# A Mamba and attention kernel: the tails of C copied by ScalarE from PSUM, and a later C product in one slot of sixteen

## The chip, the cores and the metric

One NeuronCore of a Trainium2 chip runs the whole program. The metric is the device time of one execution in microseconds, as the median of repeated runs. Five engines work side by side, each through its own instructions in order: TensorE (PE in the profile), VectorE (DVE), ScalarE (ACT), GpSimd (POOL) and SyncE (SP), which here only issues DMAs. They wait for each other through semaphores.

## The reference

Two layers over x of 4 batches, 512 channels, 64 x 64 positions (L = 4096). The second layer is a linear attention with 8 heads. The first is a group norm, a layer norm, and then, for each of 4 chunks of 128 channels, a Mamba block with 256 inner channels and 16 states:

```python
xz = einsum(x, in_proj_w); xi, z = split(xz)
xc = silu(causal_conv4(xi)); dt, Bs, Cs = split(einsum(xc, x_proj_w))
dt = softplus(einsum(dt, dt_proj_w) + dt_proj_b)
h  = exp(dt_t * A) * h + (dt_t * x_t) * B_t      # per channel and state, over t
y  = sum over states of h * C_t
y  = (y + xc * D_param) * silu(z);  out = einsum(y, out_proj_w)
```

The step that matters here is y: every state's h is multiplied with its row of C, and the 16 states are summed.

## The kernel before, in words

**Tiling.** The sequence is cut into NT = 8 tiles of T = 512 positions. A *step* n is one batch, tile and chunk: 4 x 8 x 4 = 128 steps. A step has 256 channels x 16 states = 4096 recurrences, which fill 32 scans of 128 partitions x 512 positions. On the partitions lie 32 channels times 4 states. A *slot* is two scans (SLOTS = 16 a step, 2048 in all), a *pair* of slots makes one h tile [128, 4, 512] (hs, two buffers): the even slot of the pair is jj = 0, the odd one jj = 1.

**What a slot issues** (slot, L725). GpSimd forms bx = (dt x) * B two slots ahead (drive, L717 and L721; three buffers). ScalarE forms dA = exp(dt * A) three scans ahead into three PSUM banks (decay, L708 and L713, LEAD = 3), so that decay k + 3 can start when scan k has freed its bank. VectorE scans (L739). After the first scan of an even slot the previous pair is finished: VectorE multiplies columns 0 to 383 of its h by C, in place (product, L756 and L759), which it reads from a PSUM bank; TensorE fills that bank for the next pair (c_row, L702: one selecting matmul of the bf16 parts of the C rows, CUT = 384 columns wide; one buffer) and folds the finished h over the states into y (fold_states, L761). At the end of an odd slot GpSimd saves the last column (L750) and multiplies the tail, columns 384 to 511, by C (L751). [...] its part of C comes as an SBUF tile c_sb, which four DMAs for each pair spread from DRAM (c_tail, L697, through for_states, L685; two buffers), issued one slot before the pair begins. The rows of B come in the same way, three pairs ahead (b_row, L692), and the step times and dt x in eight DMAs of 256 KB for each half step (spread, L633, at slots 1 and 9).

**Order of the work around it.** The order within each engine is the order in which the program writes the instructions. After each slot, after() (L1109) adds the other stages at fixed slots: first what later() has put off to this slot, then among others the softplus with its two ScalarE table loads at slot 3 (L1127), the gates on GpSimd at slots 1 and 9, the inputs of step n + 2 at slots 3 and 5 to 9 (inputs, L579: the convolution's matmuls and the z matmuls into banks pc and pz, evacuated by ScalarE a slot later, L592 and L608), their Silu at slot 10 (L1048: a table load, one activation over [128, 2048], and a table load back to exp), their x, B, C projection from slot 12 (mixers, L642). Between these come pieces of the layer norms, the output projection and the previous batch's attention, as long as TensorE's budget for the slot lasts.

**The C rows.** mixers puts dt, B and three copies of the C rows into one bank pd, copies B and C to SBUF and by DMA to DRAM (rows_out, L658), and splits the 384 columns that TensorE will select into three bf16 parts (L663 to L669): a copy, then twice a matmul that subtracts it and a copy of what is left.

Of the kernel before, what the change touches and what calls it, by code (L numbers as in the profile page):

```python
# [8 lines left out]
F32 = mybir.dt.float32  # L9
# [5 lines left out]
P = 128  # L15
# [9 lines left out]
def kernel(  # L25
# [60 lines left out]
    def later(n, what):  # L86

        done = []

        def both():  # L90
            what()
            done.append(True)

        if now[0] is None:
            both()
        else:
            due.append((now[0] + n, both))
        return done
# [22 lines left out]
    def mm(out_, lhsT, rhs, abreast=1, **how):  # L121

        work["mm"] += (0.25 if rhs.dtype == BF16 else 1.0) * rhs.shape[-1] / T / abreast
        nc.tensor.matmul(out_, lhsT, rhs, **how)  # L124
# [250 lines left out]
    def bc(v, n):  # L375
        return v.unsqueeze(1).to_broadcast([P, n, v.shape[-1]])
# [190 lines left out]
    def shifted_end(f, name):  # L567
        mv = small.tile([P, NC, 2], F32, tag="mv", name=f"mv_{name}", bufs=4)
        for v in range(2):
            nc.vector.tensor_reduce(mv[:, :, v], f[("sum", "square")[v]], AX.X, ALU.add)  # L570
        nc.gpsimd.tensor_scalar(mv, mv, 1.0 / L, None, ALU.mult)
        d2 = small.tile([P, NC], F32, tag="d2", name=f"d2_{name}")
        nc.gpsimd.tensor_tensor(d2, mv[:, :, 0], mv[:, :, 0], ALU.mult)
        nc.gpsimd.tensor_tensor(mv[:, :, 1], mv[:, :, 1], d2, ALU.subtract)
        nc.gpsimd.tensor_tensor(mv[:, :, 0], mv[:, :, 0], f["mv"][:, :, 0], ALU.add)
        return mv


    def inputs(f, xn, c, nm):  # L579

        xz = f["xz"] = wk.tile([P, 2, NH, T], F32, tag="xz", name=f"xz_{nm}", bufs=3)
        pc = [None] * NH

        def taps(e, ks):
            for k in ks:
                mm(
                    pc[e], w_cv[:, k, e * P : (e + 1) * P], xn[:, c, k : k + T],
                    start=(k == 0), stop=(k == NTAP - 1),
                )

        def take(e):
            nc.scalar.activation(xz[:, 0, e, :], pc[e], AF.Identity, bias=cb[:, e : e + 1])  # L592

        for e in range(NH):
            pc[e] = work_bank(f"pc_{nm}_{e}", 0)
            taps(e, range(NTAP // 2))
            yield
            taps(e, range(NTAP // 2, NTAP))
            later(1, lambda e=e: take(e))
            yield  # L600
        for e in range(NH):
            pz = work_bank(f"pz_{nm}_{e}", 0)
            mm(
                pz, w_z[:, e * P : (e + 1) * P], xn[:, c, NTAP - 1 : NTAP - 1 + T],
                start=True, stop=True,
            )

            later(1, lambda e=e, pz=pz: nc.scalar.copy(xz[:, 1, e, :], pz))  # L608
            yield

    def time_banks(f, nm):
# [30 lines left out]
    def mixers(f, nm):  # L642

        pd = work_bank(f"pd_{nm}", 0)
        for e in range(NH):
            mm(pd, w_xp[:, e, :], f["xz"][:, 0, e, :], start=(e == 0), stop=(e == NH - 1))
        yield
        f["both"] = wk.tile([P, 2, NH, T], F32, tag="dt", name=f"dt_{nm}", bufs=1)  # L650
        dtr = f["dtr"] = f["both"][0 : 2 * LANE, 1, NH - 1, :]
        nc.scalar.copy(dtr, pd[0 : 2 * LANE, :])
        b_rows = f["b_rows"] = dram.tile([NST, T], F32, tag="b_rows", name=f"b_rows_{nm}", bufs=3)
        c_rows = f["c_rows"] = dram.tile(
            [NST, T - CUT], F32, tag="c_rows", name=f"c_rows_{nm}", bufs=3
        )

        def rows_out():  # L658
            nc.sync.dma_start(b_rows, dtr[RANK : RANK + NST, :])
            nc.sync.dma_start(c_rows, dtr[LANE : LANE + NST, CUT:])  # L660

        later(1, rows_out)
        parts = f["parts"] = wk.tile([P, CUT], BF16, tag="parts", name=f"parts_{nm}", bufs=3)  # L663
        nc.scalar.copy(parts, pd[:, :CUT])
        for i in (2, 3):
            yield
            mm(pd[:, :CUT], minus, parts, start=False, stop=True, skip_group_check=True)
            yield
            nc.scalar.copy(parts[i * LANE :, :], pd[i * LANE :, :CUT])  # L669

# [12 lines left out]
    def for_states(dst, rows_, q):  # L685

        for k in range(KS):
            nc.sync.dma_start(  # L688
                dst[k * BLK : (k + 1) * BLK, :], rows_[q * KS + k, :].partition_broadcast(BLK)
            )  # L690
# [5 lines left out]

    def c_tail(g):  # L697
        n, e, q, _ = place(g)
        c_sb[g // JJ] = wk.tile([P, T - CUT], F32, tag="c_sb", name=f"c_sb_{g}", bufs=2)
        for_states(c_sb[g // JJ], fs[n]["c_rows"], q)  # L700

    def c_row(g):  # L702
        n, e, q, _ = place(g)
        got = ps_c.tile([P, CUT], F32, tag="c", name=f"c_all_{g}")
        mm(got, sel[:, q, :], fs[n]["parts"], start=True, stop=True)
        c_all[g // JJ] = got

# [17 lines left out]
    def slot(g, last, after):  # L725
        n, e, q, jj = place(g)
        b, t, c = steps[n]
        if g + 2 < last:
            drive(g + 2)
        if jj == 0:  # L730
            if g + 3 * JJ < last:
                b_row(g + 3 * JJ)
            hs[g // JJ] = wk.tile([P, NJ, T], F32, tag="h", name=f"h_{g}", bufs=2)
        elif g + 1 < last:
            c_tail(g + 1)
        h = hs[g // JJ]
        for i in range(2):
            j = jj * 2 + i
            nc.vector.tensor_tensor_scan(  # L739
                h[:, j, :], dAs.pop(2 * g + i), bxs[g][:, i, :],  # L740
                0.0 if t == 0 else st[:, c, e, q, j : j + 1], ALU.mult, ALU.add,
            )
            if 2 * g + i + LEAD < 2 * last:
                decay(2 * g + i + LEAD)
            if i == 0 and jj == 0 and g:
                product(g - 1)
                fold_states(g - 1, last)
        del bxs[g]
        if jj == JJ - 1:
            nc.gpsimd.tensor_copy(st[:, c, e, q, :], h[:, :, T - 1])  # L750
            nc.gpsimd.tensor_tensor(  # L751
                h[:, :, CUT:], h[:, :, CUT:], bc(c_sb.pop(g // JJ), NJ), ALU.mult
            )
        after()

    def product(g):  # L756

        own = hs[g // JJ][:, :, :CUT]
        nc.vector.tensor_tensor(own, own, bc(c_all.pop(g // JJ), NJ), ALU.mult)  # L759

    def fold_states(g, last):  # L761

# [43 lines left out]
    def attention(b, x1s, stats):  # L806
# [87 lines left out]

        kqn = wk.tile([P, NC, P], F32, tag="res", name=f"kqn_{b}", bufs=2)
        nc.gpsimd.memset(kqn, 0.0)
        nrm = small.tile([P, NC], F32, tag="nrm", name=f"nrm_{b}")
        nc.vector.tensor_reduce(nrm, kq, AX.X, ALU.add)
        nc.gpsimd.tensor_scalar(nrm, nrm, 1e-6, None, ALU.add)
        nc.vector.reciprocal(nrm, nrm)  # L900
# [145 lines left out]
        return inputs(fs[n], xn[b, t], c, names[n])  # L1046

    def silu(n):  # L1048
        nc.scalar.activation(fs[n]["xz"], fs[n]["xz"], AF.Silu)  # L1049

    ahead, late, rest, light = [], [], [], []

# [21 lines left out]
    silu(0)  # L1074
    run(mixers(fs[0], names[0]))
    b_row(0)
    c_tail(0)
    time_banks(fs[0], names[0])
    time_steps(fs[0], names[0])
    for v in range(2):  # L1080
# [160 lines left out]
```

## Time and profile before

| | us |
|---|---|
| runs before | 7912.8, 7906.63, 7911.72 (median 7911.72) |
| the profiled execution | 7900.44 |
| its span, first to last instruction | 7898.7 |
| busy: POOL, DVE, PE, ACT | 6894.4, 6908.9, 6434.6, 5509.8 |
| all 128 steps, first to last scan | 7301 |
| issue of one c_sb load on SP, median | 0.42 |
| c_sb load, issue to landing, median | 1.8 |

A line of a group reads: line of the kernel, engine, operation, output<-inputs, shapes, count, then busy time and the mean ns of one, then the engine's idle time just before such instructions and what ended it. Line 124 is the helper mm, through which all matmuls go, so matmuls are told apart by their tiles. In the timeline a row has the start, the duration and, in brackets, the idle time before it. Records of consecutive instructions on VectorE and ScalarE overlap by some hundredths of a microsecond. A wait for several things is put down to the one that came last.

### The profile page before, as it was taken

What the parts mean: (1) busy time and instruction counts of PE and PEld (TensorE: products, weight loads), DVE (VectorE), ACT (ScalarE), POOL (GpSimd) and SP (SyncE); (2) the same over time, 40 slices, a digit from 0 to 9 for tenths busy, and PEclk for the clock granted to TensorE, in tenths of its full rate; (3) what the DMA queues carried; (4) which work ended last, traced back from release to release, by engine and by line L of the source; (5) the groups of instructions that cost most, each with busy time, mean ns of one, the idle gap of its engine ahead of it and who ended that gap; (6) DMA issues with size and microseconds to landing.
All of it is one profiled execution on the core that took longest, in us unless ns stands there. A gap on an engine that the chain in (4) does not pass through costs nothing.

```text
span 7898.7 us, 90490 instructions
## 1 busy us (share of the span) xinstructions
PE 6434.6 (81%) x24834; PEld 2109.1 (27%) x24880; DVE 6908.9 (87%) x5650; ACT 5509.8 (70%) x8329; POOL 6894.4 (87%) x4649
## 2 busy tenths in 40 slices
PE   5676777677789888988788888888788888888599
PEld 1121212112223232322222223322122222322144
DVE  5999999999999999989999999998989999988500
ACT  4677777777777777777777777777777777777421
POOL 4999999999999999989999999999999999999500
PEclk7888888788899999999899999999889999999799
DMA  5676666666776666776766666777666666677402
GB/s 156 167 170 168 159 153 158 161 155 165 171 176 165 161 163 159 182 187 174 170 167 169 171 164 159 175 179 181 164 159 169 158 164 155 156 194 182 102 32 91
DMA packets 829184, 1265.87 MB, mean 160 GB/s; under 512 B 183912, under 2 KB 317560, under 8 KB 816384
## 3 DMA queue, kind: packets, MB, share of 16 engines
q1 hardware_dynamic: 804736, 1222.32, 61.5%
q0 software_dynamic: 16896, 33.56, 2.5%
q10 hardware_dynamic: 7040, 4.20, 0.2%
q8 instruction: 195, 3.19, 0.2%
q14 instruction: 317, 2.60, 0.1%
HBM read 1052.78 MB, written 206.57 MB: 159 GB/s over the span
## 4 chain that ended last, share of the span: by engine, by line
DVE 32%; PE 21%; DMA 13%; ACT 12%; issue 8%; POOL 7%; SPq 6%; POOLq 0%; DVEq 0%; ACTq 0%
DVE h L739 22%; DVE h L759 9%; DMA d_all<-d_rows 7%; PE pq L124 5%; POOL bx L721 5%; ACT dA L713 4%; PE pc L124 4%; SPq L688 3%; PE y L124 3%; PE pr L124 2%; SPq L639 2%; PE po L124 2%; DMA c_sb<-c_rows 2%; ACT xz L1049 2%; DMA b_all<-b_rows 2%
## 5 line engine op out<-in xcount | busy, mean ns | idle before, releaser
L721 POOL TENSOR_TENSOR bx<-d_all,b_all 128x1024 f32<-128x1024 f32 x2048 | 4824.4, 2369 | 157.7 <-DVE h L739 141.3
L739 DVE TENSOR_TENSOR_SCAN h<-dA,st,bx 128x512 f32<-128x512 f32 x3584 | 4358.0, 1264 | 372.5 <-ACT dA L713 164.4
L713 ACT ACTIVATE dA<-d_all,a_t 128x512 f32<-128x512 f32 x4096 | 2754.3, 687 | 1501.3 <-DVE h L739 1444.7
L759 DVE TENSOR_TENSOR h<-h,c_all 128x1536 f32<-128x1536 f32 x1024 | 1767.6, 1726 | 0.1
L751 POOL TENSOR_TENSOR h<-h,c_sb 128x512 f32<-128x512 f32 x1024 | 1301.1, 1271 | 227.2 <-DMA c_sb<-c_rows 125.1
L124 PE MATMUL y<-h,fold 128*32 128x512 f32 x8192 | 1271.6, 697 | 93.2 <-POOL h L751 88.6
L124 PE MATMUL c_all<-parts,sel 128*128 128x384 bf16 x1024 | 368.3, 360 | 1073.2 <-DVE h L759 1071.0
L124 PE MATMUL pc<-xn,w_cv 128*128 128x512 f32 x2048 | 1037.4, 640 | 118.7 <-DVE xn L414 63.9
L124 PE MATMUL pq<-w_qk,xa 128*128 128x512 f32 x2048 | 963.8, 604 | 7.8 <-issue 4.9
L739 DVE TENSOR_TENSOR_SCAN h<-dA,bx 128x512 f32<-128x512 f32 x512 | 591.8, 1204 | 88.5 <-ACT dA L713 62.7
L124 PEld LDWEIGHTS <-sel 128*128 128x128 bf16 x1280 | 126.8, 99 | 1716.1 <-DVE h L759 1519.5
L124 PEld LDWEIGHTS pc<-xn,w_cv 128*128 128x128 f32 x2048 | 386.5, 199 | 736.4 <-issue 418.0
L124 PEld LDWEIGHTS pq<-w_qk,xa 128*128 128x128 f32 x2048 | 396.6, 195 | 443.7 <-issue 425.4
L124 PE MATMUL pr<-xb,m 128*128 128x512 f32 x1024 | 481.8, 608 | 12.3 <-DMA xb<-x 7.0
L124 PE MATMUL pp<-xn,w_pr 128*128 128x512 f32 x1024 | 477.9, 597 | 4.8 <-DVE xn L414 4.8
L124 PEld LDWEIGHTS y<-h,fold 128*32 128x32 f32 x8192 | 170.3, 114 | 661.9 <-issue 322.4
L124 PE MATMUL y<-xz,dg 32*32 32x512 f32 x2048 | 335.8, 731 | 0.0
L781 POOL TENSOR_TENSOR xz<-xz 128x512 f32<-128x512 f32 x256 | 325.9, 1273 | 5.9 <-ACT xz L778 5.8
L832 ACT ACTIVATE kq<-pq 128x512 f32<-128x512 f32 x256 | 150.6, 588 | 253.3 <-PE pq L124 252.5
L124 PE MATMUL pd<-xz,w_xp 128*128 128x512 f32 x512 | 318.3, 753 | 7.8 <-ACT xz L1049 7.8
L628 POOL TENSOR_TENSOR dt<-dt,xz 128x1024 f32<-128x1024 f32 x128 | 302.5, 2363 | 22.5 <-ACT dt L620 22.5
L124 PE MATMUL pz<-xn,w_z 128*128 128x512 f32 x512 | 273.2, 625 | 9.7 <-ACT xz L608 8.2
(177 smaller groups left out, 5981.2 us busy)
## 6 DMA issues: line engine op xcount, KB each, us to landing
d_all<-d_rows SPq DMA_DIRECT2D x2048, 256.0 KB, 6.6
b_all<-b_rows SPq DMA_DIRECT2D x4096, 64.0 KB, 2.2
d_rows<-dt SPq DMA_DIRECT2D x256, 512.0 KB, 3.7
c_sb<-c_rows SPq DMA_DIRECT2D x4096, 16.0 KB, 1.8
xs<-in_x_dram SPq DMA_DIRECT2D x32, 1024.0 KB, 6.1
xn<-in_x_dram SPq DMA_DIRECT2D x32, 1024.0 KB, 6.2
xr<-in_x_dram POOLq DMA_DIRECT2D x32, 1024.0 KB, 10.2
x<-xr SPq DMA_DIRECT2D x32, 1024.0 KB, 4.2
```

What stands on the lines that cost most here:

```text
L124: nc.tensor.matmul(out_, lhsT, rhs, **how)
L628: nc.gpsimd.tensor_tensor(f["both"][:, 1], f["both"][:, 0], f["xz"][:, 0], ALU.mult)
L639: nc.sync.dma_start(d[k * BLK : (k + 1) * BLK, v], src)
L688: nc.sync.dma_start(dst[k * BLK : (k + 1) * BLK, :], rows_[q * KS + k, :].partition_broadcast(BLK))
L713: nc.scalar.activation(dAs[k], fs[n]["d_all", e][:, 0, j, :], AF.Exp, scale=a_t[:, e, j, q : q + 1])
L721: nc.gpsimd.tensor_tensor(bxs[g], fs[n]["d_all", e][:, 1, jj * 2 : jj * 2 + 2, :], bc(b_all[g // JJ], 2), ALU.mult)
L739: nc.vector.tensor_tensor_scan(h[:, j, :], dAs.pop(2 * g + i), bxs[g][:, i, :], 0.0 if t == 0 else st[:, c, e, q, j : j + 1], ALU.mult, AL ...
L751: nc.gpsimd.tensor_tensor(h[:, :, CUT:], h[:, :, CUT:], bc(c_sb.pop(g // JJ), NJ), ALU.mult)
L759: nc.vector.tensor_tensor(own, own, bc(c_all.pop(g // JJ), NJ), ALU.mult)
L781: nc.gpsimd.tensor_tensor(f["xz"][:, 1, e, :], f["xz"][:, 1, e, :], f["xz"][:, 0, e, :], ALU.mult)
L832: nc.scalar.activation(qk[i], pq, AF.Relu)
L1049: nc.scalar.activation(fs[n]["xz"], fs[n]["xz"], AF.Silu)
```

## The change

Four things. The parts of C, their subtracting matmuls and the selecting matmul become 512 columns wide, so that the bank c_all holds the whole row. c_tail becomes one ScalarE copy of columns 384 to 511 of that bank to c_sb (one buffer), issued in the pair's own odd slot behind the decay that follows its first scan; the DRAM tile c_rows, its write and the four loads for each pair go. At slot 10 of each step the product and the fold of the pair before are issued behind the slot's second scan. The second z bank is not copied to SBUF any more: Silu is done in two activations, over the three quarters that lie in SBUF and from the bank. Three small buffers become single.

```diff
@@ -569,7 +569,7 @@
         for v in range(2):
             nc.vector.tensor_reduce(mv[:, :, v], f[("sum", "square")[v]], AX.X, ALU.add)
         nc.gpsimd.tensor_scalar(mv, mv, 1.0 / L, None, ALU.mult)
-        d2 = small.tile([P, NC], F32, tag="d2", name=f"d2_{name}")
+        d2 = small.tile([P, NC], F32, tag="d2", name=f"d2_{name}", bufs=1)
         nc.gpsimd.tensor_tensor(d2, mv[:, :, 0], mv[:, :, 0], ALU.mult)
         nc.gpsimd.tensor_tensor(mv[:, :, 1], mv[:, :, 1], d2, ALU.subtract)
         nc.gpsimd.tensor_tensor(mv[:, :, 0], mv[:, :, 0], f["mv"][:, :, 0], ALU.add)
@@ -605,7 +605,9 @@
                 start=True, stop=True,
             )
 
-            later(1, lambda e=e, pz=pz: nc.scalar.copy(xz[:, 1, e, :], pz))
+            if e + 1 < NH:
+                later(1, lambda e=e, pz=pz: nc.scalar.copy(xz[:, 1, e, :], pz))
+            f["pz"] = pz
             yield
 
     def time_banks(f, nm):
@@ -651,22 +653,18 @@
         dtr = f["dtr"] = f["both"][0 : 2 * LANE, 1, NH - 1, :]
         nc.scalar.copy(dtr, pd[0 : 2 * LANE, :])
         b_rows = f["b_rows"] = dram.tile([NST, T], F32, tag="b_rows", name=f"b_rows_{nm}", bufs=3)
-        c_rows = f["c_rows"] = dram.tile(
-            [NST, T - CUT], F32, tag="c_rows", name=f"c_rows_{nm}", bufs=3
-        )
 
         def rows_out():
             nc.sync.dma_start(b_rows, dtr[RANK : RANK + NST, :])
-            nc.sync.dma_start(c_rows, dtr[LANE : LANE + NST, CUT:])
 
         later(1, rows_out)
-        parts = f["parts"] = wk.tile([P, CUT], BF16, tag="parts", name=f"parts_{nm}", bufs=3)
-        nc.scalar.copy(parts, pd[:, :CUT])
+        parts = f["parts"] = wk.tile([P, T], BF16, tag="parts", name=f"parts_{nm}", bufs=3)
+        nc.scalar.copy(parts, pd)
         for i in (2, 3):
             yield
-            mm(pd[:, :CUT], minus, parts, start=False, stop=True, skip_group_check=True)
+            mm(pd, minus, parts, start=False, stop=True, skip_group_check=True)
             yield
-            nc.scalar.copy(parts[i * LANE :, :], pd[i * LANE :, :CUT])
+            nc.scalar.copy(parts[i * LANE :, :], pd[i * LANE :, :])
 
 
 
@@ -696,12 +694,12 @@
 
     def c_tail(g):
         n, e, q, _ = place(g)
-        c_sb[g // JJ] = wk.tile([P, T - CUT], F32, tag="c_sb", name=f"c_sb_{g}", bufs=2)
-        for_states(c_sb[g // JJ], fs[n]["c_rows"], q)
+        c_sb[g // JJ] = wk.tile([P, T - CUT], F32, tag="c_sb", name=f"c_sb_{g}", bufs=1)
+        nc.scalar.copy(c_sb[g // JJ], c_all[g // JJ][:, CUT:])
 
     def c_row(g):
         n, e, q, _ = place(g)
-        got = ps_c.tile([P, CUT], F32, tag="c", name=f"c_all_{g}")
+        got = ps_c.tile([P, T], F32, tag="c", name=f"c_all_{g}")
         mm(got, sel[:, q, :], fs[n]["parts"], start=True, stop=True)
         c_all[g // JJ] = got
 
@@ -731,8 +729,6 @@
             if g + 3 * JJ < last:
                 b_row(g + 3 * JJ)
             hs[g // JJ] = wk.tile([P, NJ, T], F32, tag="h", name=f"h_{g}", bufs=2)
-        elif g + 1 < last:
-            c_tail(g + 1)
         h = hs[g // JJ]
         for i in range(2):
             j = jj * 2 + i
@@ -742,7 +738,9 @@
             )
             if 2 * g + i + LEAD < 2 * last:
                 decay(2 * g + i + LEAD)
-            if i == 0 and jj == 0 and g:
+            if i == 0 and jj == JJ - 1:
+                c_tail(g)
+            if i == int(g % SLOTS == AWAY[1]) and jj == 0 and g:
                 product(g - 1)
                 fold_states(g - 1, last)
         del bxs[g]
@@ -756,7 +754,7 @@
     def product(g):
 
         own = hs[g // JJ][:, :, :CUT]
-        nc.vector.tensor_tensor(own, own, bc(c_all.pop(g // JJ), NJ), ALU.mult)
+        nc.vector.tensor_tensor(own, own, bc(c_all.pop(g // JJ)[:, :CUT], NJ), ALU.mult)
 
     def fold_states(g, last):
 
@@ -894,7 +892,7 @@
 
         kqn = wk.tile([P, NC, P], F32, tag="res", name=f"kqn_{b}", bufs=2)
         nc.gpsimd.memset(kqn, 0.0)
-        nrm = small.tile([P, NC], F32, tag="nrm", name=f"nrm_{b}")
+        nrm = small.tile([P, NC], F32, tag="nrm", name=f"nrm_{b}", bufs=1)
         nc.vector.tensor_reduce(nrm, kq, AX.X, ALU.add)
         nc.gpsimd.tensor_scalar(nrm, nrm, 1e-6, None, ALU.add)
         nc.vector.reciprocal(nrm, nrm)
@@ -1046,7 +1044,9 @@
         return inputs(fs[n], xn[b, t], c, names[n])
 
     def silu(n):
-        nc.scalar.activation(fs[n]["xz"], fs[n]["xz"], AF.Silu)
+        xz = fs[n]["xz"].rearrange("p i e t -> p (i e) t")
+        nc.scalar.activation(xz[:, : 2 * NH - 1], xz[:, : 2 * NH - 1], AF.Silu)
+        nc.scalar.activation(xz[:, 2 * NH - 1], fs[n]["pz"], AF.Silu)
 
     ahead, late, rest, light = [], [], [], []
 
@@ -1074,7 +1074,6 @@
     silu(0)
     run(mixers(fs[0], names[0]))
     b_row(0)
-    c_tail(0)
     time_banks(fs[0], names[0])
     time_steps(fs[0], names[0])
     for v in range(2):
```

## The prediction

> **What bounds the kernel now.** I read the busy table by stretch first (the start, the four batches, the tail), then the waits of VectorE and GpSimd inside the loop, then the groups, then a timeline of one step. The first view shows which engine can set the pace.
>
> ```profile
> core 0: us, PE busy (x) PEld busy (x) DVE busy (x) ACT busy (x) POOL busy (x), PEclk, DMA share, GB/s
> ...
> 123.00:1886.00 1763.00, 1257.32 (x4680) 339.79 (x4679) 1702.74 (x1354) 1282.57 (x1916) 1709.03 (x1142) 0.82 0.67 162
> 1886.00:3735.00 1849.00, 1570.10 (x6198) 521.95 (x6208) 1723.53 (x1402) 1373.85 (x2083) 1722.53 (x1161) 0.93 0.68 170
> ...
> 7424.00:7899.00 475.00, 431.91 (x1494) 198.24 (x1510) 20.21 (x49) 103.87 (x167) 9.83 (x18) 0.93 0.17 58
> ```
>
> In the loop (7301 us, 128 steps of 57.0 us) VectorE and GpSimd are both busy for 93 to 97%; the tail of 475 us is the last batch's attention and the change does not touch it. Two engines that full wait for each other, and what can be won or lost is their idle time, some 450 us each. The waits say where it lies (us in total, times, longest):
>
> ```profile
> DVE h L739 <- ACT dA L713: 227.1, 188, 46.4
> DVE h L739 <- PE y L124: 91.6, 87, 4.1
> DVE h L739 <- POOL bx L721: 90.5, 79, 4.6
> ...
> POOL bx L721 <- DVE h L739: 141.3, 228, 3.6
> POOL h L751 <- DMA c_sb<-c_rows: 125.1, 81, 5.7
> POOL st L750 <- DVE h L739: 33.7, 52, 2.2
> POOL h L751 <- DMA b_all<-b_rows: 14.2, 8, 2.9
> ```
>
> VectorE waits most for ScalarE's decays, and GpSimd for VectorE and for the C tails' DMAs (the last line is such a wait put down to its neighbour in the queue: 139.3 us in 89 waits in all). Sorting the scans' idle times by slot (scan k belongs to slot k/2): 75 us lie before the second scan of slot 5, behind the softplus table loads, and 62 us before the second scan of slot 12, behind Silu. The tails' idle times, sorted alike, are 57 us at slot 5 and 88 us at slot 13; some 8 us of each is a constant 0.06 us step between L750 and L751.
>
> The durations used:
>
> ```profile
> L739 DVE TENSOR_TENSOR_SCAN h<-dA,st,bx 128x512 f32<-128x512 f32 x3584 | 4358.0, 1264 | 372.5 <-ACT dA L713 164.4
> L713 ACT ACTIVATE dA<-d_all,a_t 128x512 f32<-128x512 f32 x4096 | 2754.3, 687 | 1501.3 <-DVE h L739 1444.7
> L759 DVE TENSOR_TENSOR h<-h,c_all 128x1536 f32<-128x1536 f32 x1024 | 1767.6, 1726 | 0.1
> L751 POOL TENSOR_TENSOR h<-h,c_sb 128x512 f32<-128x512 f32 x1024 | 1301.1, 1271 | 227.2 <-DMA c_sb<-c_rows 125.1
> ...
> L124 PE MATMUL c_all<-parts,sel 128*128 128x384 bf16 x1024 | 368.3, 360 | 1073.2 <-DVE h L759 1071.0
> ```
>
> And ScalarE around slots 10 to 12 of one step:
>
> ```profile
> 4056.07 0.69 ACT L713 ACTIVATE dA<-d_all,a_t 128x512 f32<-128x512 f32 x1 [0.42 <-DVE h L739]
> 4056.70 0.58 ACT L608 COPY xz<-pz 128x512 f32<-128x512 f32 x1
> 4057.29 1.28 ACT L1049 ACT_TABLE_LOAD   x1
> 4058.59 1.91 ACT L1049 ACTIVATE xz<-xz 128x2048 f32<-128x2048 f32 x1
> 4060.52 1.28 ACT L1150 ACT_TABLE_LOAD   x1
> 4061.81 0.72 ACT L473 ACTIVATE sq_b<-xn,about 128x512 f32<-128x512 f32 x1
> 4062.44 1.28 ACT L713 ACTIVATE dA<-d_all,a_t 128x512 f32<-128x512 f32 x2
> ```
>
> From the decay of slot 10 to the next one ScalarE is away for 5.7 us; VectorE's product of slot 12 began at 4061.00, and its next scan had to wait for the decay until 4063.14.
>
> [...]
>
> **The change, part by part.**
>
> *DMAs out.* 4096 loads of c_sb, 128 writes of c_rows. On SP that is 4224 times 0.42 us, but SP's own time ends no wait of a computing engine except the tails', 139 us. What such a wait is worth I read from the trace: over the 93 steps of the later batches, a least-squares fit of a step's length on the waits in it gives 1.0 us per us waited at slot 5, but 0.2 to 0.6 at slot 13. So 49 + 0.5 x 80 + 10 for the other slots: **100 us saved** (bounds 50 and 139).
>
> *Copies in.* 1024 copies of 0.25 us, 260 us of ScalarE, and 3 x 128 part copies by 0.11 us more (41 us); against that one copy fewer per step (74 us) and a Silu in two (19 us more, the fixed part of an instruction). ScalarE goes from 70% to some 73%. Behind the copy in its queue stand the next decays. Adding the time to every stretch in which ScalarE worked without a pause, up to the next pause, makes only 10 us of decays later than their scans: **10 us lost**, the rest lies in ScalarE's 1445 us of waits for VectorE. The copy itself waits for the C rows' matmul and for the one c_sb buffer: by the trace's times 9 us in all.
>
> *The copy as a wait.* It stands behind decay 2g+3 of an odd slot g. For each pair I set the end of that decay plus 0.33 us (copy and semaphore) against the start of the tail on GpSimd and of the product on VectorE. Tails: later than now by 366 us in sum, half of it at slot 11, where the copy stands behind Silu; but each of these delays fits into the lead of the bx product that follows it (2.7 us in the median at slot 14), up to 1 us in all, so I take 0 for it by itself. Products: these read the same bank as the copy. If the reads are ordered as they stand in the code, the product of slot 12 waits for a copy that stands behind Silu. In the step above, after the change: scans at 4053.1, decay 24 behind decay 23 at 4055.6, Silu's three parts from 4056.3 to 4061.0, sq_b, decay 25 and the copy to 4062.6. So the product starts 1.6 us later than its 4061.00 and the scan behind it at some 4064.3 instead of 4063.14. Over 126 steps the waits sum to 145 us at slot 12, 46 at slot 6, 19 at slot 8, 13 at slot 2 and 2 elsewhere: 225 us. The bounds are 0 (nothing orders the reads) and 225. I take the ordered case.
>
> *Slot 10 and Silu.* With the product behind the second scan, decay 24 starts by 0.9 us earlier in the mean (0 to 1.6, less where decay 23 is late), and some 0.4 us go with the dropped copy. The 62 us at slot 12 vanish: decay 25 now ends before the copy for which the product waits anyway. This is counted in the 145. The fold of slot 10 ends up to 1.2 us later; against the trace's gaps it makes 11 us before slot 12's first scan. The pz bank is held until Silu has read it, 1 to 3 us longer; TensorE may wait for it (0 to 10 us; I take 0, for TensorE then waits for the product).
>
> *The rest.* Matmuls of 512 instead of 384 columns: 0.38 against 0.34 us by the bias rows' matmul of the same kind (pq<-bqk in the timeline), 1280 x 0.04 = 51 us on a TensorE that waits 1071 us for that same product: 0. Buffer counts of d2 and nrm: small tiles, once a batch: 0.
>
> *Sum.* The new waits less the old one are 225 - 62 = 163 us on VectorE; of a wait at slot 12 the same fit lets 0.6 to 0.9 reach the end, since VectorE later waits less for GpSimd. 0.7 x 163 = 114. Then 114 + 10 + 0.7 x 11 - 100 = +32 us. The profiled execution took 7900.4 us (span 7898.7 and 1.7 around it), which makes 7932; it lies 11.3 us below the median of the runs, so on that scale **7944**, 0.4% slower.
>
> **The rivals.** (1) *Faster*: the product does not wait for the copy, or VectorE's delay is swallowed because GpSimd is the true bound and now starts its tails in time. For it: GpSimd is busy 97% in the first batch, and slot 5's DMA wait costs its full length. [...] Time: -100 - 0.7 x 62 + 18 = -125 at best; with GpSimd's late tails taking half of that, -60: 7850. It decides as soon as under some 70 us of the 225 reach the end. (2) *No change*: both sums meet; 7912. (3) *ScalarE becomes the bound*: copies in front of the decays in slots 3 to 6 and 10 to 13 cost their 0.25 us each time, 8 a step, 4 of them in full: 128 x 1.0 = 128 us on top: 8070. Against it: its idle time of a quarter of the loop.
>
> **How the numbers follow.** Forecast 0.39 and rival 3 0.08 are slower; rival 1 0.36 is faster; rival 2 0.17 (within 0.2%, 16 us, which is about what a measurement of this kernel tells from no change). The range runs from 7810, between rival 1's 7850 and its best of 7787, to 8030, the forecast with all 163 us at the end and three quarters of the saving: 7912 + 163 + 28 - 75. The forecast's own range is 7920 to 8030.
>
> **What would show it.** GpSimd's waits for c_sb's DMA are gone. VectorE's L759, which never waited (0.1 us), waits for ScalarE's copy by some 150 to 225 us, two thirds at slot 12; the 62 us at the second scan of slot 12 are gone. GpSimd waits for the same copy at slot 11. If L759 still has no idle time, the ordering step is wrong and the time falls to rival 1; if the waits are there and the time falls all the same, the slack was mis-sized; if waits for dA grow by over 50 us, it is rival 3.

## The result and the profile after

| | before | after |
|---|---|---|
| median of the runs, us | 7910.11 (7906.63 to 7912.8, 4 runs) | 8017.08 (8013.05 to 8018.2, 4 runs) |
| the profiled execution, its span | 7900.44, 7898.7 | 8013.05, 8011.4 |
| all 128 steps, first to last scan | 7301 | 7418 |
| busy: POOL, DVE, PE, ACT | 6894.4, 6908.9, 6434.6, 5509.8 | 6889.8, 6924.3, 6564.8, 5671.9 |

The changed kernel is slower by 107 us: the ratio is 1.0134, with a 95% interval of 1.0122 to 1.0147. The start is 4.6 us shorter and the tail is the same (474 us), so everything lies in the loop: 117 us, 0.9 us a step. Granted clocks are close (0.901 before, 0.897 after) and not the cause: the kernel e14 below took 7860.89 us at 0.897.

The busy table by stretch of the changed kernel, for the first two of the four batches (the columns are named in its first line):

```profile
core 0: us, PE busy (x) PEld busy (x) DVE busy (x) ACT busy (x) POOL busy (x), PEclk, DMA share, GB/s
...
118.00:1911.00 1793.00, 1312.42 (x4680) 341.94 (x4680) 1706.88 (x1353) 1319.66 (x2170) 1711.16 (x1143) 0.81 0.63 150
1911.00:3794.00 1883.00, 1597.35 (x6195) 523.33 (x6208) 1727.35 (x1402) 1415.50 (x2339) 1722.12 (x1161) 0.92 0.64 158
```

VectorE's and GpSimd's busy time is what it was, within some 4 us a batch; the batches are 30 and 34 us longer. Between the first and the last scan VectorE's idle time went from 451 to 553 us and GpSimd's from 428 to 548, so nearly all of the loss is idle time of both. VectorE's waits say how its idle time was rearranged (us in total, times, longest):

```profile
...
DVE h L735 <- PE y L124: 178.9, 164, 3.0
DVE h L735 <- ACT dA L711: 151.9, 96, 42.6
DVE h L757 <- ACT c_sb L698: 149.3, 144, 4.1
...
DVE h L735 <- POOL bx L719: 12.8, 19, 1.9
```

Two waits shrank: ScalarE's decays from 227 to 152 us, GpSimd's bx from 91 to 13. Two grew: the product waits for the copy by 149 us where it had none, and the scans wait for TensorE to finish y, that is, to release h, by 179 instead of 92. VectorE's waits for the attention's matmuls inside the loop grew by 29 us too. GpSimd's waits:

```profile
...
POOL h L749 <- ACT c_sb L698: 225.0, 176, 3.6
...
POOL bx L719 <- DVE h L735: 51.6, 108, 2.0
```

No wait for a c_sb load is left, but the tail now waits for ScalarE by 225 us where it had waited for DMAs by 139. GpSimd's bx products wait for VectorE by 90 us less. The groups concerned (before: 0.1 us of idle time at the product, 227.2 at the tail):

```profile
L757 DVE TENSOR_TENSOR h<-h,c_all 128x1536 f32<-128x1536 f32 x1024 | 1776.2, 1735 | 151.5 <-ACT c_sb L698 149.3
L749 POOL TENSOR_TENSOR h<-h,c_sb 128x512 f32<-128x512 f32 x1024 | 1302.0, 1271 | 428.6 <-ACT c_sb L698 225.0
L124 PE MATMUL c_all<-parts,sel 128*128 128x512 bf16 x1024 | 429.9, 420 | 1137.5 <-DVE h L757 1136.0
```

Slots 10 to 12 of one step, first ScalarE's timeline (start, duration):

```profile
3944.39 1.28 ACT L1048 ACT_TABLE_LOAD   x1
3945.68 1.49 ACT L1048 ACTIVATE xz<-xz 128x1536 f32<-128x1536 f32 x1
3947.07 0.58 ACT L1049 ACTIVATE xz<-pz 128x512 f32<-128x512 f32 x1
3947.67 1.28 ACT L1149 ACT_TABLE_LOAD   x1
3948.97 0.69 ACT L711 ACTIVATE dA<-d_all,a_t 128x512 f32<-128x512 f32 x1
3949.59 0.26 ACT L698 COPY c_sb<-c_all 128x128 f32<-128x128 f32 x1
```

and then VectorE's (in brackets the idle time before the row):

```profile
3947.47 1.22 DVE L735 TENSOR_TENSOR_SCAN h<-dA,bx 128x512 f32<-128x512 f32 x1 [0.20 <-PE y L124]
3949.89 1.75 DVE L757 TENSOR_TENSOR h<-h,c_all 128x1536 f32<-128x1536 f32 x1 [1.20 <-ACT c_sb L698]
```

The scan of slot 12 ends at 3948.69. Its product has all that it computes with, but waits 1.20 us for a copy of 0.26 us that ends at 3949.85, behind two table loads, two activations and a decay. Summed over the 128 steps, the idle time at slot 12 is 84, 107 and 0 us before the first scan, the product and the second scan; before the change it was 53, 0 and 61. Slots 6 and 8 have 19 and 17 us at the product. The tail's idle time at the odd slots 1, 3, ... 15 went from 17, 12, 57, 15, 12, 11, 88, 15 us to 66, 10, 29, 59, 65, 163, 16, 19: slots 5 and 13, where the DMAs came late, are better by 100 us; slots 1, 7, 9 and 11 are worse by 298, and 152 of these stand at slot 11, behind Silu.

### The profile page after: what moved, and what is told of

Same layout as the page of the kernel before. It is cut to its first block, busy times and chain, and to the rows that moved or that the text cites. A ratio compares the mean times of both kernels' runs of the same rounds, so it can differ in the third digit from the quotient of the medians.

```text
span 8011.4 us, 86934 instructions
## 1 busy us (share of the span) xinstructions
PE 6564.8 (82%) x24827; PEld 2121.9 (26%) x24880; DVE 6924.3 (86%) x5650; ACT 5671.9 (71%) x9353; POOL 6889.8 (86%) x4649
## 4 chain that ended last, share of the span: by engine, by line
PE 30%; DVE 26%; ACT 22%; issue 11%; POOL 6%; DMA 4%; SPq 1%; DVEq 0%; POOLq 0%; ACTq 0%
DVE h L735 15%; DVE h L757 9%; ACT dA L711 9%; PE pq L124 6%; PE pc L124 5%; PE y L124 5%; POOL bx L719 4%; PE pr L124 3%; PE po L124 3%; DMA d_all<-d_rows 2%; PE pp L124 2%; ACT L1048 1%; ACT L1149 1%; PE pd L124 1%; PE c_all L124 1%
## 5 line engine op out<-in xcount | busy, mean ns | idle before, releaser
L711 ACT ACTIVATE dA<-d_all,a_t 128x512 f32<-128x512 f32 x4096 | 2802.6, 690 | 1391.5 <-DVE h L735 1351.4
L757 DVE TENSOR_TENSOR h<-h,c_all 128x1536 f32<-128x1536 f32 x1024 | 1776.2, 1735 | 151.5 <-ACT c_sb L698 149.3
L124 PE MATMUL c_all<-parts,sel 128*128 128x512 bf16 x1024 | 429.9, 420 | 1137.5 <-DVE h L757 1136.0
L124 PE MATMUL y<-xz,dg 32*32 32x512 f32 x2048 | 359.3, 779 | 0.0
L837 DVE TENSOR_TENSOR kq<-pk,kq 128x256 f32<-128x256 f32 x124 | 51.4, 415 | 268.5 <-PE pk L124 268.1
```

The source lines that it names most:

```text
L711: nc.scalar.activation(dAs[k], fs[n]["d_all", e][:, 0, j, :], AF.Exp, scale=a_t[:, e, j, q : q + 1])
L757: nc.vector.tensor_tensor(own, own, bc(c_all.pop(g // JJ)[:, :CUT], NJ), ALU.mult)
L837: nc.vector.tensor_tensor(kq, pk, kq, ALU.add)
```

## The experiments

The theory: the copy orders the two readers of the C bank, so that the product (and the tail) wait for ScalarE's queue, and this costs more than the DMAs did. The rivals: the loss is ScalarE's or TensorE's added work (wider rows, 1024 copies); or it is the move of slot 10. A time in us is a median, and "against before" is against the kernel before in runs on the same chip. Each ratio to the kernel before has its 95% interval. Medians of two kernels can come from different series of runs, in which the kernel before took 7906.52 to 7915.72 us, so differences between them are loose by up to some 10 us.

### e1: the move of slot 10 alone

In the kernel before, only:

```diff
-            if i == 0 and jj == 0 and g:
+            if i == int(g % SLOTS == AWAY[1]) and jj == 0 and g:
```

> The kernel before with one edit of the change: at slot 10 the product behind the second scan. Theory (the copy as a wait): this part alone hides Silu, so the 62 us before the second scan of slot 12 go, and the later fold takes some 30 of them back: 7880 to 7910. Rival (TensorE's late folds): with only two scans between the product of slot 10 and the h tile's next use, VectorE waits for y at slot 12 by 50 us more: 7930 to 7960.

Measured: 7903.36, ratio 0.9987 (0.9979 to 0.9996), as expected. The wait before slot 12's second scan falls from 61 to 22 us, that before its first scan rises from 53 to 78. The move is no cost, and by itself hardly a gain: what it takes from one scan it gives in large part to another, since the fold that it delays has to release h. The prediction had 11 us for that, and it is 25: the pair folded in slot 10 is the first of its half step, and the matmuls that add xc * D to y stand between its c_row and its fold.

### e3 and e4: the changed kernel without the move, and without the split Silu

e3 takes the line of e1 back in the changed kernel; e4 copies the second z bank again and does one Silu.

> The changed kernel with the product of slot 10 back behind the first scan. Theory: Silu and with it the copy for slot 12's product come 0.9 us later per step, and only what the fold loses comes back: 8030 to 8070. Rival: the folds come in time again: 7970 or less.

> The changed kernel with the second z bank copied by ScalarE and one Silu over all, as before. Theory: the copy behind Silu comes 0.4 us later in each step and the product of slot 12 with it: 0.7 x 0.4 x 128 = 36 us more, 8050. Rival: no change, 8010 to 8025.

Measured: e3 8118.1, ratio 1.0258 (1.0244 to 1.0272); e4 8072.66, ratio 1.0201 (1.0187 to 1.0215). VectorE's and GpSimd's largest waits of e3:

```profile
DVE h L757 <- ACT c_sb L698: 289.7, 211, 4.7
```

```profile
POOL h L749 <- ACT c_sb L698: 285.9, 181, 4.0
```

Without the move the product of slot 12 waits for 235 us instead of 107, and the kernel is 101 us slower than the change, above the range expected. The same line was worth 11 us in the kernel before. e4 is 56 us slower than the change, where 36 were expected: the product of slot 12 waits for 152 us. Here nothing but the moment at which ScalarE comes back from Silu is changed, and the time follows it about one to one: 0.43 us a step (a z copy less what the second activation costs) times 128 is 55 us. The move and the split Silu are thus no part of the loss: without either one it is larger.

### e5 to e8: who waits for the copy

Four kernels cut the two waits apart. In e5 ScalarE copies a constant from SBUF to c_sb, so that the tails still wait for the copy but the product does not; in e6 the tails multiply with a constant; e7 does both; e8 is e7 with C's parts, subtracting matmuls and selecting matmul 384 columns wide again. Copies are made in all of them; those from SBUF take 287 ns instead of 264, so the kernels without a wait spare ScalarE no work. The core of e5 and of e6:

```diff
-        nc.scalar.copy(c_sb[g // JJ], c_all[g // JJ][:, CUT:])
+        nc.scalar.copy(c_sb[g // JJ], w_z[:, : T - CUT])
...
-                h[:, :, CUT:], h[:, :, CUT:], bc(c_sb.pop(g // JJ), NJ), ALU.mult
+                h[:, :, CUT:], h[:, :, CUT:], bc(w_z[:, : T - CUT], NJ), ALU.mult
```

> The changed kernel, in which ScalarE's copy reads a constant SBUF tile (w_z) in place of the C rows' bank, so that VectorE's product has no copy to wait for; the tails still wait for the copy, and are multiplied with those constants in place of C. Theory (the product behind the copy, which passes to the end in full): the 149 us of L757's waits go and some 25 us before the second scan of slot 12 come back: 7880 to 7910. Rival A (the tails behind the copy on GpSimd): at most a third of it, 7970 to 8017. Rival B (TensorE's folds): VectorE's waits for y stay at 180 us or grow, 7950.

> The changed kernel, in which the tails are multiplied with a constant SBUF tile (w_z) in place of the copied C, so that GpSimd waits for no copy; the copies are made and the product waits for them as in the changed kernel. Theory: 8000 to 8020, GpSimd's 225 us of waits cost next to nothing. Rival A: 7930 or less.

> Both edits together: the copy reads a constant tile and the tails use a constant tile in place of C, so ScalarE's 1024 copies gate nobody and only their time is left. Theory: 7860 to 7900, the kernel before less the DMA waits and the Silu stall. Rival C (ScalarE's added time makes decays late): 7950 or more.

> As the one with both edits, and the C parts and the matmuls 384 columns wide again. The difference to it is the price of the wider rows alone. Theory: under 15 us. Rival B: 40 us or more, with VectorE's waits for y smaller by as much.

| | us | ratio (95%) | against before, us |
|---|---|---|---|
| the change: both wait | 8017.08 | 1.0134 (1.0122 to 1.0147) | +107 |
| e6: only the product waits | 8006.98 | 1.0110 (1.0097 to 1.0124) | +91 |
| e5: only the tails wait | 7941.77 | 1.0028 (1.0017 to 1.0040) | +26 |
| e7: neither waits | 7868.13 | 0.9938 (0.9924 to 0.9952) | -48 |
| e8: neither waits, 384 columns | 7836.12 | 0.9897 (0.9883 to 0.9910) | -80 |

e6 and e7 came out as expected, e5 (7880 to 7910) and e8 (at most 15 us under e7) did not. The main question is settled all the same. With every copy and every wide row in place but no one waiting for the copy, the kernel is 48 us faster than before. The two waits cost 149 us (8017 - 7868), 155 on the scale of the last column. In e5 and e7 the product has no idle time, and in e6 the tails have only the constant step before them:

```profile
L757 DVE TENSOR_TENSOR h<-h,c_all 128x1536 f32<-128x1536 f32 x1024 | 1774.9, 1733 | 0.1
```

```profile
L749 POOL TENSOR_TENSOR h<-h,w_z 128x512 f32<-128x512 f32 x1024 | 1300.5, 1270 | 82.6 <-POOL st L748 0.4
```

(the first line is e7's, the second e6's). So of the 429 us before the tails in the changed kernel some 346 hang on the copy, more than the 225 that are put down to it by name. The product's wait alone costs 139 us, nine tenths of its 152.7 us of idle time in e6. The tails' wait alone costs 74 us, and on top of the product's only 10: they are no sum. The likely reason is that product and tail wait for the same late copy. In e5 the idle time of VectorE shows how a late tail comes back:

```profile
DVE h L735 <- PE y L124: 195.6, 170, 3.0
DVE h L735 <- ACT dA L711: 131.4, 146, 3.6
DVE h L735 <- POOL bx L719: 103.7, 73, 44.0
```

The scans wait for y's fold (which needs the tail) and for the bx product that is queued behind the tail on GpSimd: 196 and 104 us, against 140 and 55 in e7 (44 and 46 of the bx waits are the very first scan's):

```profile
DVE h L735 <- PE y L124: 139.9, 130, 3.0
DVE h L735 <- ACT dA L711: 127.8, 130, 3.4
DVE h L735 <- POOL bx L719: 54.6, 13, 45.7
```

That is rival B of e5's expectation, late folds: of the 196 us, 56 go when the tails wait no longer. And the width, which the prediction had at nothing, costs 32 us (e7 less e8).

### e9, e11 and e15: the same copy, earlier in ScalarE's queue

e11 moves the copy from the pair's odd slot to its even one, behind c_row, the fold and the slot's second decay, and puts the product at slot 10 back behind the first scan. e9 puts the product back too, but moves only the copy of the pair of slots 10 and 11; e15 moves the seven other copies, and leaves the product of slot 10 behind the second scan. The edit of e11:

```diff
-            if i == 0 and jj == JJ - 1:
-                c_tail(g)
-            if i == int(g % SLOTS == AWAY[1]) and jj == 0 and g:
+            if i == 0 and jj == 0 and g:
                 product(g - 1)
                 fold_states(g - 1, last)
+            if (i, jj) == (1, 0):
+                c_tail(g)
```

> The changed kernel with the product of slot 10 behind the first scan again and, for the pair of slots 10 and 11 alone, the copy in slot 10 behind its second decay, that is in front of Silu. Theory (a copy that stands behind Silu): the 107 us of the product's waits at slot 12 and GpSimd's long wait at slot 11 go, the folds of slot 10 come 1.2 us earlier, and some 30 us of Silu's stall before the second scan of slot 12 come back: 7880 to 7930. Rival (any copy on ScalarE costs this much, wherever it stands): 7980 or more.

> The changed kernel with the product of slot 10 behind the first scan and every pair's copy in its even slot behind the second decay. No product waits for a copy any more, but ScalarE now waits for the C rows' matmul where TensorE is late (1 to 2 us in the mean at slots 2 to 6). Theory: between the early copy of one slot alone and 40 us above it, 7900 to 7960. Rival: as there or faster.

> The changed kernel with every pair's copy in its even slot behind the second decay, but for the pair of slots 10 and 11, whose copy stays behind Silu, and with the product of slot 10 moved as in the changed kernel. What is left of the waits is the one copy behind Silu. If that one is two thirds of the cost of the waits (149 us): 8017 less 40 to 60, 7957 to 7977. If the other seven carry most of it: 7930 or less.

Measured: e9 7941.15, ratio 1.0038 (1.0025 to 1.0051), slightly above its range; e11 7927.19, ratio 1.0019 (1.0011 to 1.0027); e15 7970.9, ratio 1.0078 (1.0066 to 1.0091), both within their ranges. The product's waits of e9, then of e15:

```profile
DVE h L757 <- ACT c_sb L698: 57.2, 94, 1.8
```

```profile
DVE h L757 <- ACT c_sb L698: 108.2, 76, 4.0
```

In e9 none of them is at slot 12, where the second scan waits for its decay by 81 us instead; in e15 all are at slot 12. So the place of the copies in the queue is worth 90 of the 107 us. Moving the copy that stands behind Silu, together with the product of slot 10 back behind the first scan, gives 76 us if the others stay (the change against e9) and 44 if the seven others are early already (e15 against e11); no run moves it alone. Moving these seven gives 46 and 14. Like the two waits of e5 and e6, they are no sum. e11 was expected at or above e9 and came out below it, so the seven early copies are a gain there too. In e11 the product has no idle time and the tail 117 us instead of 429:

```profile
L757 DVE TENSOR_TENSOR h<-h,c_all 128x1536 f32<-128x1536 f32 x1024 | 1772.1, 1731 | 0.1
L749 POOL TENSOR_TENSOR h<-h,c_sb 128x512 f32<-128x512 f32 x1024 | 1300.4, 1270 | 117.0 <-ACT c_sb L698 37.2
```

What is late next is seen in ScalarE's waits of e11:

```profile
ACT c_sb L698 <- PE c_all L124: 254.1, 208, 3.5
```

The copy now comes before its input and holds ScalarE for the C rows' matmul, by 254 us in 208 waits; in the changed kernel that matmul itself waits for the product on VectorE, by 1136 us, and the copy's waits for it are 8 us, as the prediction's 9 had it. e11 is still 59 us above e7, where no one waits.

### e10: the change's other two edits, in the kernel before

The move of slot 10 and the split Silu, with the DMAs kept.

> The kernel before with the two edits of the change that have nothing to do with C's tails: the product of slot 10 behind the second scan, Silu partly from PSUM. Theory: 7903 of the first edit alone, less some 15 us of the 22 that were left before the second scan of slot 12: 7880 to 7900. Rival: no gain over the first edit.

Measured: 7896.68, ratio 0.9983 (0.9976 to 0.9990), as expected. The two edits gain 16 us where nothing depends on a copy.

### e12 and e13: the D term's matmuls ahead of the moved product

In both, the matmuls of xc * D are issued in slots 1 and 9, not in front of the folds of slots 2 and 10; e12 is the changed kernel with this edit, e13 is e10 with it.

```diff
+            if i == 0 and jj == JJ - 1 and q == 0:
+                ys[n, e] = ps_y.tile([P, T], F32, tag="y", name=f"y_{n}_{e}")
+                diagonal(ys[n, e], dg[:, e, :], fs[n]["xz"][:, 0, e, :])
...
-        if q == 0:
-            ys[n, e] = ps_y.tile([P, T], F32, tag="y", name=f"y_{n}_{e}")
-            diagonal(ys[n, e], dg[:, e, :], fs[n]["xz"][:, 0, e, :])
```

> The changed kernel with the eight matmuls that open a half step's y bank (the D term, from dg) issued in slots 1 and 9, behind the first scan, in place of directly in front of the fold at slots 2 and 10. They need nothing of h, so the fold of slot 10 ends some 1.1 us sooner behind its product. Theory (ScalarE's copy sets when the product of slot 12 starts): the waits for y before slot 12's first scan fall from 84 us to under 30, but the product's wait for the copy grows by most of that: 7985 to 8010. Rival B (the folds are the larger cost): 7960 or less.

> The kernel before with the product of slot 10 moved, Silu partly from PSUM, and the D term's matmuls issued early; no copies on ScalarE. Nothing here waits for a copy, so the 80 us of waits for y before slot 12's first scan should turn into time: 7897 less 30 to 60, 7835 to 7870. Rival (GpSimd's throughput is the bound): 7885 or more.

Measured: e12 8029.85, ratio 1.0148 (1.0134 to 1.0162); e13 7926.28, ratio 1.0023 (1.0016 to 1.0030). Both expectations missed. VectorE's waits of e12:

```profile
DVE h L760 <- ACT c_sb L698: 229.4, 170, 5.0
...
DVE h L735 <- PE y L124: 115.2, 92, 4.1
```

At slot 12 the first scan's wait does fall, from 84 to 8 us, but the product's rises from 107 to 181: their sum stays (191, 188). The two are in series in front of one event, the copy: as long as the copy comes when it did, an earlier scan only makes the product wait longer. That e12 is 13 us slower and not level is not explained by this. In e13 there is no copy; slot 12's first scan does gain (80 to 27 us), yet the waits at slots 0, 8, 10 and 12's second scan grow by 16, 13, 7 and 19. The matmuls also changed TensorE's budget (the program's own count of matmul work for each slot) in some slots, and with it which piece of other work comes where; whether that is what costs the 30 us is open.

### e14, e16, e17 and e18: why width costs

Wide rows with the DMAs kept (e2) do not fit into SBUF: the pool wk needs 170.19 KB a partition, where 169.69 are left. So the width has a price only in kernels without these DMAs. e14 is e7 with a selecting matmul of 384 columns and parts of 512. In the other three all rows are 512 wide but the budget that spreads the other work over the slots counts them as 384: e16 in e7, e17 in the changed kernel, e18 in e11.

```diff
-    def mm(out_, lhsT, rhs, abreast=1, **how):
+    def mm(out_, lhsT, rhs, abreast=1, counted=None, **how):
...
-        work["mm"] += (0.25 if rhs.dtype == BF16 else 1.0) * rhs.shape[-1] / T / abreast
+        work["mm"] += (0.25 if rhs.dtype == BF16 else 1.0) * (counted or rhs.shape[-1]) / T / abreast
...
-            mm(pd, minus, parts, start=False, stop=True, skip_group_check=True)
+            mm(pd, minus, parts, counted=CUT, start=False, stop=True, skip_group_check=True)
...
-        mm(got, sel[:, q, :], fs[n]["parts"], start=True, stop=True)
+        mm(got, sel[:, q, :], fs[n]["parts"], counted=CUT, start=True, stop=True)
```

> As the kernel with both edits (copies and tails from constant tiles, 7868), with the C parts 512 columns wide but the selecting matmul 384 columns wide as before. The wider rows cost 32 us together, which the prediction took at nothing. If it is the selecting matmul, 8 a step in front of the folds: 7836 to 7845. If it is ScalarE's three wider part copies and the two subtracting matmuls: 7860 to 7870.

> As the kernel with both edits (copies and tails from constant tiles, rows 512 columns wide, 7868), but with the wider matmuls counted at 384 columns in the budget that spreads the other stages over the slots, so that the pieces come in the slots in which they came with narrow rows. If the wider rows cost by their own time on ScalarE or TensorE: 7860 to 7875. If they cost by the order of the pieces that the budget makes of them: 7836 to 7848.

> The changed kernel with the same edit of the budget. If the order of the pieces is what the wider rows cost: 8017 less some 30, 7980 to 7995. If not: 8010 to 8020.

> The kernel with every pair's copy in its even slot (7927), with the same edit of the budget; nothing is left out. If the order is the cause: 7890 to 7905, a little below the kernel before; if not: 7920 to 7935.

Measured: e14 7860.89, ratio 0.9937 (0.9924 to 0.9951); e16 7863.75, ratio 0.9946 (0.9934 to 0.9958); e17 7975.76, ratio 1.0092 (1.0077 to 1.0106); e18 7897.02, ratio 0.9986 (0.9980 to 0.9993). Each came out at one of the values that it was to tell apart, e17 4 us below its range. Where no one waits for the copy (e7 7868, e14, e16), neither the wide selecting matmul nor the order of the pieces shows a cost clear of noise: 25 of the 32 us (31 against before) stay with the wide parts and the matmuls that subtract them. Where the copy gates (by the medians 41 us for e17 against the changed kernel, 30 for e18 against e11; by the ratios 33 and 26), the order of the other pieces is worth as much as the width itself. So the price of the two waits depends on that order: with the budget counted at 384 columns they cost 112 us (e17 less e16), with the changed kernel's own budget 149 (the change less e7). Why the order matters only where the copy gates stays open.

e18 does all of the computation with C's tails from PSUM and is faster than the kernel before by 0.14%. e10 and e1, which keep the DMAs, are faster by 0.17% and 0.13%. These are the only three whole kernels here that beat it, each by less than 0.2%.

## Why the prediction was right or wrong

The direction and the main mechanism, a product held by the copy behind Silu, were right; the size was not: the sum was +32 us and the measurement +107. The steps that failed are the other terms of the sum. The wider rows, put at nothing, cost 32 us; the gain from the DMAs was put at 90 us net of the copies and is 64; that from slot 10 and Silu was put at 35 and is 16. Together these are more than the 75 us that were missing. On the scale of differences from the kernel before (each with some 10 us of interval either way), the terms stand like this:

| term | predicted | measured | from |
|---|---|---|---|
| the move and the split Silu, the wait at slot 12's second scan gone, the later fold | -43 + 8 | -16 | e10 |
| DMAs out, copies' time in | -100 + 10 | -64 | e8 less e10 |
| wider rows | 0 | +32 | e7 less e8 |
| tails and product behind the copy | 0.7 x 225 = +157 | +155 | the change less e7 |
| sum | +32 | +107 | |

The measured column adds up by construction, since each line is a step between two kernels; in another order of steps the shares would differ. With the budget counted at 384 columns the last line would be +112 (e17 less e16).

**The copy as a wait: right.** L757, which never waited, waits 149 us in 144 waits, 107 us of them at slot 12, and the 62 us at its second scan are gone, as the prediction said they would be. That it waits because both read one bank, in the order of the code, was the author's assumption, one of two cases; e5 bears it out: when the copy reads another tile, the product's 149 us of waits are gone. The 0.33 us that the prediction allowed for the copy and the semaphore were an estimate: in these 144 waits the product starts 0.22 to 0.24 us after the end of the decay in front of the copy. e7, 48 us faster than before with every copy made, shows that the waits for the copies make the loss, not the copies' own time. The term's 157 agrees with 155 partly by luck. The wait is 149 us and not 225: slots 12 and 6 have 107 and 19 instead of 145 and 46, and at slot 12 the difference lies before the first scan, which now waits 84 us instead of 53. But each us of it cost 0.9 in e6, and from the change to e3 and e4 140 and 45 us more of it cost 101 and 56, that is 0.7 and 1.2: the prediction's 0.7 lies at the lower end. And the tails, which were to fit into the lead of bx "up to 1 us in all, so I take 0", cost 74 us by themselves (e5) and 10 on top of the product (16 against before): the 0 fails as a statement on the tail, and does little harm in the sum.

**Width: wrong, a term of the sum at nothing.** "51 us on a TensorE that waits 1071 us for that same product: 0". The selecting matmul took 0.420 us instead of 0.360, and e14 agrees that it is hidden. But the parts' copies on ScalarE went from 0.473 to 0.580 us (the first line is from before, the second from the changed kernel):

```profile
L669 ACT CAST parts<-pd 64x384 bf16<-64x384 f32 (+1 forms) x256 | 121.1, 473 | 9.5 <-PE pd L124 3.3
...
L667 ACT CAST parts<-pd 64x512 bf16<-64x512 f32 (+1 forms) x256 | 148.4, 580 | 8.4 <-PE pd L124 2.3
```

With the two matmuls that subtract them they cost 25 of the 32 us (e14 less e8). The prediction had these copies' 41 us in ScalarE's total, where it found slack for them; they stand in a chain from slot 12 on, behind Silu, which is the likely place of the loss, though no run here shows it there. It also left out that the wider matmuls count more in TensorE's budget, and so move other pieces: nothing in e7 (e16), 33 to 41 us in the changed kernel (e17).

**DMAs out: right in sign, too large.** 139 us of waits were taken as 100; with the copies' own time the gain is 64. GpSimd's waits for a DMA vanish, but in e7, where no tail waits, GpSimd's bx waits for VectorE by 205 us instead of 141: what it wins on one side it waits for on the other. The weight of 0.5 at slot 13 had little to stand on: a fit with the waits at slots 5, 12 and 13, over 93 steps of the same trace, gives that slot from -0.3 to 0.7, by the slot at which a step is taken to begin, with a standard error of 0.2. Whether the missing 26 us lie there, no run separates. The copies are about as short as predicted: 264 ns each, against 0.25 us. The trace before gives nearly the same as an estimate: ScalarE takes 473 ns for 384 columns (L669) and 580 for 512 (L608), thus 107 for each 128 columns, which makes 259 for 128.

**Slot 10 and Silu: right in direction, too large.** -35 against -16. The fold's delay was put at 11 us and is 25 (e1), since the D term's matmuls before it were not in the working; with them out of the way (e12, e13) the wait before slot 12's first scan falls from 84 to 8 and from 80 to 27 us. That the pz bank is held longer was taken at 0, and in the changed kernel no wait of a z matmul is put down to the Silu that now reads that bank.

**The rivals.** Rival 1 (the product does not wait) is refuted for the change, and e5 shows that it would not have been faster either: tails alone make it 26 us slower than before. Its price of -125 us at best is not reached even by e8, -80. Rival 2, no change, falls with the interval. Rival 3, ScalarE as the bound, would have been near the time (8070), but its sign is missing: the decays' waits did not grow by 50 us, they fell by 75, and in e7 all the copies fit in. The weight lies on the order in ScalarE's queue, above all behind Silu, not on its load (71%).

## What to carry to other kernels

When a small operation is moved to an engine with slack, ask where in that engine's queue it stands, and what the engine does there: here a copy of 0.26 us behind a Silu that takes 4.6 us with its two table loads set the time of a product that needed nothing from it, and putting that copy and its seven neighbours earlier in the queue gave back 90 of 107 us. Two engines read one PSUM bank here in the order of the code, and that order was a wait for the other engine's queue: 149 us for VectorE's product, and a us of it cost 0.7 to 1.2 us. Between two engines that are both about 95% busy, the 139 us of DMA waits gave back half of their length and the product's added waits cost most of theirs; and two waits in front of one event did not add (191 us together at slot 12, 188 with the first all but gone), so that removing the first (e12) gave nothing.

## What was not expected of the hardware and the program

- Wider casts: 128 more columns of a cast from PSUM cost ScalarE 107 ns (473 to 580 ns, with 64 or 128 partitions), and the matmul with bf16 operands 60 ns (360 to 420), where the prediction estimated 40 from another matmul.
- The same ScalarE copy of 128 columns took 264 ns from PSUM (the changed kernel) and 287 ns from SBUF (e7).
- The move of one product by one scan was worth 11 us in one kernel and 101 in the other (e1, e3). What this edit was worth depended on what was late beside it.
